# Attention's values, queries and keys as seven products of quarters in place of eight

## The chip, the cores and the metric

The kernel runs on one core of one Trainium2 chip. A core has five engines that run side by side and wait for each other on semaphores: TensorE for matrix products (PE in the profile, its weight loads PEld), VectorE (DVE), ScalarE (ACT), GpSimd (POOL) and SyncE (SP), which here only issues transfers. The metric is the device time of one execution in microseconds (us), less being better.

## The reference, cut to what matters

Two parts follow each other: a graph layer (two rounds of attention over edges) and a transformer block (dense attention, then a mixture of experts). The change touches the dense attention and its border to the graph layer.

```python
def _attention(x, Wqkv, Wproj):          # x: 1 x 1250 x 768, 12 heads of 64
    qkv = (x @ Wqkv).reshape(B, T, 3, H, HD)
    q, k, v = (qkv[:, :, 0], qkv[:, :, 1], qkv[:, :, 2])
    scores = jnp.einsum('bqhd,bkhd->bhqk', q, k) * jnp.float32(HD) ** (-0.5)
    attn = jax.nn.softmax(scores, axis=-1)
    out = jnp.einsum('bhqk,bkhd->bqhd', attn, v).reshape(B, T, D)
    return out @ Wproj
...
x = x + L0_gnn_ref(layernorm(x), ...)          # graph layer
x = x + L0_ffn_ref(layernorm(x)[None], ...)[0]  # x = x + attention(ln1(x)); x = x + moe(ln2(x))
```

All data are float32.

## The kernel before

The 1250 rows are `NT = 10` tiles of `T = 125`, the 768 features `DC = 6` chunks of `P = 128`. A float32 matmul is recorded as two passes of PE.

**End of the graph layer.** `gat_layer(2, ...)` yields row tile after row tile. For each, DVE adds the residual (`xres`), takes two layer norms and leaves `y`; PE turns `y` into six chunks of columns (`ptr`, line 146), and ACT writes them with the norm's scale and offset into `yT` (6 chunks x 1250 columns, in the slot "A" of the pool `big`; slot "B" holds the graph layer's `h`, later the values `v`). With tile 0 the values' weight `wv` (768 x 768) is loaded into the pool `wpool`, which has one buffer. The edge counts `cnt` are read by DVE when it makes the weights `wt` (line 522); PE reads `wt` and `h` in the aggregation (line 529).

**Before the first unit.** POOL fills `zero` and issues nine transfers that clear the table `xd`, which the experts need much later (lines 621 to 627). `value_rows(t)` makes the values of one row tile: two halves of 384 columns, six matmuls each, in a two-bank PSUM tile, copied by ACT (line 663). `queries_keys(p)` makes queries and keys of a pair of heads: it loads the two weight slices `wqk` on SP's queue, and for each of three column chunks of 417 or 416 makes six matmuls for keys (bank `mb`) and six for queries (bank `pz`); ACT copies them into `qk`, scaling the queries by 1/8. It is a generator with one matmul per step. PE's order is written out here (`manual_schedule`): two value tiles, all of pair 0's queries and keys, then the scores of the first unit in turn with the eight other value tiles.

**The units.** A unit is a pair of heads (6) and a third of the queries (3), 18 in all. `Unit.scores(j)` makes the scores of key tile `j` for both heads in a two-bank tile `st` (two buffers); ACT copies them into one of 15 buffers `sT`, DVE keeps the running maximum `most`. `top` and `row` turn the maxima by PE (`ptop`, DVE's reduction `m`, then `mb`). `weights(j)` subtracts on DVE, takes the exponential on ACT, and POOL adds the weights up in `acc`. `values(j)` multiplies with `v` into `pav`. One unit later `divide` sums `acc` over partitions into `pz`, copies `pav` into `aT`, and sends the sums by SP's queue through memory (`zd`, `z`); `invert` takes the reciprocals on DVE and fetches them as `rz` (line 765), and yet a unit later `scale` multiplies on POOL. Only the last unit divides directly. PE's order inside a unit is written out: two steps of the next pair's queries and keys, `top`, `divide`, four steps, the next unit's scores 0, `row`, and then for every two key tiles two scores, two steps (the first three times), and two values. So each of the first fifteen units carries twelve matmuls of the next pair. DVE, ACT, POOL and the transfers are ordered by a planner, apart from instructions pinned with `keep_in_program_order`.

**After the units.** `wp`, the output projection's weight, is loaded into `wpool` once `wv` is done with. `xs`, the rows saved in memory, takes slot "A" after `yT`; its loads alternate between SP's and ACT's queue (line 953). `product(t)` projects row tile `t` (`po`).

Of the kernel before, what the change touches and what calls it, by code (L numbers as in the profile page):

```python
# [10 lines left out]
F32 = mybir.dt.float32  # L11
# [16 lines left out]
def gnn_ffn_kernel(  # L28
# [137 lines left out]
    with tc.tile_pool(name="cnt", bufs=1) as cpool:  # L166
# [277 lines left out]
        with tc.tile_pool(name="gwork", bufs=2) as gp, \  # L444
# [142 lines left out]
            for t, o in gat_layer(2, all_of_second, gb2):  # L587
                if t == 0:
                    yT = big.tile([P, DC, N], F32, tag="A", name="yT")
                    wv = wpool.tile([P, DC, D], F32, tag="w", name="wv")  # L590
                    nc.sync.dma_start(wv, Wqkv[:, 2 * D:3 * D].rearrange("(c p) f -> p c f", p=P))
                xr = gp.tile([T, D], F32, tag="xr", name="xres")
                nc.sync.dma_start(xr, x[t * T:(t + 1) * T, :])
                nc.vector.tensor_add(xr, xr, o)
                nc.scalar.dma_start(xsd[t * T:(t + 1) * T, :], xr)
                mean, rstd = ln_stats(xr)
                nc.vector.tensor_copy(st0[:, 0, t:t + 1], mean)
                nc.vector.tensor_copy(st0[:, 1, t:t + 1], rstd)
                y = gp.tile([T, D], F32, tag="row", name="y")
                ln_apply(y, xr, mean, rstd)  # L600
                mean, rstd = ln_stats(y)
                ln_apply(y, y, mean, rstd)
                transpose_rows(gpt, y, affine(yT, t, 0))


    attn = late.enter_context(tc.tile_pool(name="attn", bufs=1))
    aT = attn.tile([P, DC, N], F32, name="aT")
    with tc.tile_pool(name="att", bufs=2) as ap, \
            tc.tile_pool(name="aps", bufs=2, space=PSUM) as aps, \
            tc.tile_pool(name="apm", bufs=1, space=PSUM) as apm, \  # L610
            tc.tile_pool(name="apa", bufs=1, space=PSUM) as apa:
        heads = [slice(i * HD, (i + 1) * HD) for i in range(2)]
# [4 lines left out]
        def pair_psum(name):  # L617
            return aps.tile([P, 2, 512], F32, tag="s", name=name)


        zero = ap.tile([P, RW], F32, name="zero", bufs=1)
        nc.gpsimd.memset(zero, 0.0)  # L622
        nc.gpsimd.memset(zero[:, D:D + 1], float(NOWHERE))
        for e in range(NE):
            nc.gpsimd.dma_start(xd[e * REG:(e + 1) * REG, :].rearrange("(p r) d -> p r d", p=P),
                                zero[:, None, :].to_broadcast([P, REG // P, RW]))
        nc.gpsimd.dma_start(xd[NOWHERE:NOWHERE + P, :], zero)

        def queries_keys(p):

            wqk = ap.tile([P, DC, 2, P], F32, tag="wqk", name="wqk", bufs=1)
            for i in (1, 0):
                nc.sync.dma_start(wqk[:, :, i, :], Wqkv[:, i * D + p * P:i * D + (p + 1) * P].rearrange(
                    "(c p) f -> p c f", p=P))
            qk = ap.tile([P, 2, N], F32, tag="qk", name="qk")
            yield qk
            for c0, w in CHUNKS:
                for i in (1, 0):
                    if i == 1:
                        pq = apm.tile([P, 2, 512], F32, tag="mb", name="pk")[:, 0, :]  # L640
                    else:
                        pq = apa.tile([P, 512], F32, tag="pz", name="pq")
                    for c in range(DC):
                        nc.tensor.matmul(pq[:, :w], wqk[:, c, i, :], yT[:, c, c0:c0 + w],  # L644
                                         start=(c == 0), stop=(c == DC - 1))
                        if c == DC - 1:
                            nc.scalar.mul(qk[:, i, c0:c0 + w], pq[:, :w], 1.0 if i == 1 else HD ** -0.5)
                        yield None

# [3 lines left out]

        v = big.tile([T, NT, D], F32, tag="B", name="v")

        def value_rows(t):
            pv = pair_psum("pv")
            for s in range(2):
                for c in range(DC):
                    nc.tensor.matmul(pv[:T, s, :DH], yT[:, c, t * T:(t + 1) * T],  # L660
                                     wv[:, c, s * DH:(s + 1) * DH],
                                     start=(c == 0), stop=(c == DC - 1))
            nc.scalar.copy(v[:, t, :].rearrange("p (s d) -> p s d", s=2), pv[:T, :, :DH])

# [8 lines left out]
        def inverses(n):  # L673
            return ap.tile([P, ZW], F32, tag="rz", name="rz")

        class Unit:


            def __init__(self, p, k, qk):
                self.p, self.qk = p, qk  # L680
                self.c0, self.w = CHUNKS[k]
                self.starts = [min(b * BW, self.w - BW) for b in range(NB)]
                self.s = []

            def scores(self, j):
                w = self.w
                st = pair_psum("st")
                for i, r in enumerate(heads):
                    nc.tensor.matmul(st[:T, i, :w], self.qk[r, 1, j * T:(j + 1) * T],  # L689
                                     self.qk[r, 0, self.c0:self.c0 + w], start=True, stop=True)  # L690
                s = ap.tile([T, 2, CW], F32, tag="sT", name="sT", bufs=15)
                nc.scalar.copy(s[:, :, :w], st[:T, :, :w])  # L692
                self.s.append(s)
                if j == 1:
                    self.most = ap.tile([T, 2, CW], F32, tag="most", name="most")
                if j > 0:
# [20 lines left out]
            def weights(self, j):  # L717
                w, s = self.w, self.s[j]
                nc.vector.tensor_tensor(s[:, :, :w], s[:, :, :w], self.mb[:T, :, :w], ALU.subtract)  # L719
                nc.scalar.activation(s[:, :, :w], s[:, :, :w], AF.Exp)  # L720
                if j == 1:
# [47 lines left out]

        steps = queries_keys(0)  # L770
        qks = [next(steps)]
        wp = load_big_weight(Wproj, "wp")
        BEFORE = 2
        with tc.manual_schedule(engines={mybir.EngineType.PE}):
            for t in range(BEFORE):
                value_rows(t)
            for _ in steps:
                pass
            u = Unit(0, 0, qks[0])
            for j in range(NT):  # L780
                u.scores(j)
                if j + BEFORE < NT:
                    value_rows(j + BEFORE)
        units = [(p, k) for p in range(DC) for k in range(NCK)]
        steps = last = None
        waiting = []
        for n, (p, k) in enumerate(units):
            if k == 0:
                steps = None
                if p + 1 < DC:  # L790
                    steps = queries_keys(p + 1)
                    qks.append(next(steps))
            nxt = Unit(*units[n + 1], qks[units[n + 1][0]]) if n + 1 < len(units) else None
            u.ns = NT if nxt is not None else NS
            with tc.manual_schedule(engines={mybir.EngineType.PE}):

                go(steps, 2)
                u.top()
                if last is not None:
                    last.divide(n - 1)  # L800
                for old in waiting:
                    old.scale()
                go(steps, DC - 2)
                if nxt is not None:
# [4 lines left out]
                for j in range(0, NT, 2):  # L809
# [3 lines left out]
                    if j < 6:  # L813
                        go(steps, 2)
                    for i in range(2):
# [388 lines left out]
```

## Time and profile before

| | us |
|---|---|
| median of three runs | 1516.32 (1513.6 to 1520.47) |
| profiled execution | 1515.23 |
| its span, first to last instruction | 1513.5 |
| end of the aggregation to the first unit | 555.5 to 671.7 |
| first fifteen units | 671.7 to 1106 |
| last three units | 1106 to 1177 |

The mean granted clock of TensorE was 0.967 over the span and 1.00 from 560 to 1200 us. Lines of the page that show the sizes of the work concerned (line, engine, operation, output and inputs, shapes, count, then busy us and mean ns of one, then the engine's idle time before them):

```profile
L725 POOL TENSOR_TENSOR acc<-acc,sT 125x834 f32<-125x834 f32 (+1 forms) x139 | 272.9, 1963 | 10.9
...
L644 PE MATMUL pq<-yT,wqk 128*128 128x417 f32 (+1 forms) x216 | 88.1, 534 | 0.0
...
L644 PE MATMUL pk<-yT,wqk 128*128 128x417 f32 (+1 forms) x216 | 84.0, 526 | 0.0
...
L660 PE MATMUL pv<-wv,yT 128*125 128x384 f32 x240 | 79.9, 490 | 1.4 <-issue 1.4
```

The counts are passes, two for a matmul. The three products take 252 us of PE. A mean of one pass includes its drain, which overlaps the next pass; the pace is read from start to start.

### The profile page before, as it was taken

The page shows a single profiled execution, that of the slowest core. Times are in us where ns is not written, and L with a number is a line of the kernel's source. Part 1 is how long each engine was busy: PE and PEld are TensorE (multiplying, and loading weights), DVE is VectorE, ACT ScalarE, POOL GpSimd, SP SyncE. Part 2 cuts the span into 40 slices and gives each one's busy share as a digit, 9 for nine tenths or more (in the row PEclk, how much of TensorE's full clock was granted, in tenths as well). Part 3 has the DMA queues.
Part 4 walks back from the last instruction along what each step waited for, and adds up shares of the span by engine and source line. Part 5 has one row for each costly group of instructions (what it writes and reads, how often), then busy time and mean ns, then how long its engine had stood idle before and what let it go on. Part 6 is the DMA issues. An engine that isn't in the chain of part 4 may idle for free. (4 is left out here: it accounts for less than half of the span.)

```text
span 1513.5 us, 16154 instructions
## 1 busy us (share of the span) xinstructions
PE 1431.7 (95%) x5990; PEld 782.7 (52%) x5990; DVE 756.8 (50%) x1271; ACT 590.3 (39%) x949; POOL 435.2 (29%) x295
## 2 busy tenths in 40 slices
PE   6787999999999999999999999999988999899997
PEld 4584655556555555553344344434333666665654
DVE  6598455435036650117766766766777654111111
ACT  4220613205026521126656656665667123221211
POOL 5000000000000001005765765775676212222222
PEclk9758999999999999999999999999999999899999
DMA  7000020000021119940100101010040323665653
GB/s 208 21 2 11 11 73 0 0 23 10 0 99 45 62 58 382 379 172 1 34 7 6 33 7 28 7 33 7 6 114 10 137 102 137 230 228 172 225 190 122
DMA packets 55578, 128.43 MB, mean 85 GB/s; under 512 B 10797, under 2 KB 29585, under 8 KB 55498
## 3 DMA queue, kind: packets, MB, share of 16 engines
q1 hardware_dynamic: 38846, 61.18, 12.6%
q0 software_dynamic: 11968, 56.21, 10.2%
q10 hardware_dynamic: 4684, 9.99, 2.2%
q8 instruction: 48, 0.79, 0.2%
q14 instruction: 32, 0.26, 0.1%
HBM read 74.17 MB, written 57.66 MB: 87 GB/s over the span
## 5 line engine op out<-in xcount | busy, mean ns | idle before, releaser
L725 POOL TENSOR_TENSOR acc<-acc,sT 125x834 f32<-125x834 f32 (+1 forms) x139 | 272.9, 1963 | 10.9
L529 PE MATMUL pagg<-h,wt 125*125 125x385 f32 (+1 forms) x800 | 263.5, 486 | 0.4 <-DVE wt L522 0.4
L719 DVE TENSOR_TENSOR sT<-sT,mb 125x834 f32<-125x834 f32 (+1 forms) x180 | 174.5, 1013 | 73.9 <-PE mb L714 73.9
L529 PEld LDWEIGHTS pagg<-h,wt 125*125 125x125 f32 x800 | 147.0, 187 | 104.7 <-DVE wt L522 3.5
L698 DVE TENSOR_TENSOR most<-most,st 125x834 f32<-125x834 f32 (+1 forms) x144 | 147.0, 1021 | 105.5 <-ACT sT L692 102.2
L720 ACT ACTIVATE sT<-sT 125x834 f32<-125x834 f32 (+1 forms) x180 | 158.1, 900 | 43.5 <-DVE sT L719 43.0
L692 ACT COPY sT<-st 125x834 f32<-125x834 f32 (+1 forms) x180 | 151.3, 848 | 42.3 <-PE st L689 38.0
L689 PE MATMUL st<-qk 64*125 64x417 f32 (+1 forms) x720 | 162.5, 551 | 5.3 <-DVE most L698 5.2
L733 PE MATMUL pav<-sT,v 125*64 125x417 f32 (+1 forms) x720 | 149.5, 527 | 8.0 <-ACT sT L720 8.0
L622 POOL MEMSET zero<- 128x771 f32 x1 | 0.7, 741 | 530.7 <-PE ptr L146 530.7
L725 POOL TENSOR_TENSOR acc<-sT 125x834 f32<-125x834 f32 (+1 forms) x18 | 35.3, 1963 | 256.5 <-ACT sT L720 256.5
L689 PEld LDWEIGHTS st<-qk 64*125 64x125 f32 x720 | 55.9, 182 | 98.8 <-DVE most L698 52.5
L733 PEld LDWEIGHTS pav<-sT,v 125*64 125x64 f32 x720 | 42.4, 135 | 103.7 <-issue 42.8
L938 PE MATMUL poe<-we,hT 128*128 128x384 f32 x264 | 89.8, 486 | 0.0
L644 PE MATMUL pq<-yT,wqk 128*128 128x417 f32 (+1 forms) x216 | 88.1, 534 | 0.0
L967 PE MATMUL po<-wp,aT 128*125 128x384 f32 x240 | 87.0, 497 | 0.0
L905 PE MATMUL phe<-xT,we 128*128 128x384 f32 (+1 forms) x288 | 86.6, 460 | 0.0
L644 PE MATMUL pk<-yT,wqk 128*128 128x417 f32 (+1 forms) x216 | 84.0, 526 | 0.0
L209 PE MATMUL ph<-gw,xnT 128*125 128x384 f32 x240 | 81.7, 500 | 1.1 <-DMA gw<-in_L_gnn_W_dram 1.1
L660 PE MATMUL pv<-wv,yT 128*125 128x384 f32 x240 | 79.9, 490 | 1.4 <-issue 1.4
L209 PE MATMUL ph<-gw,x1T 128*125 128x384 f32 x240 | 78.6, 488 | 0.0
L533 DVE RECIPROCAL rz<-pagg 125x1 f32<-125x1 f32 x20 | 3.3, 166 | 141.4 <-PE pagg L529 141.4
(230 smaller groups left out, 1699.9 us busy)
## 6 DMA issues: line engine op xcount, KB each, us to landing
xd<-zero POOLq DMA_DIRECT2D x8, 3855.0 KB, 50.2
we<-in_L_ffn_W_dram SPq DMA_DIRECT2D x16, 1152.0 KB
xr<-xd SPq DMA_DIRECT2D x25, 385.5 KB
gw<-in_L_gnn_W_dram SPq DMA_DIRECT2D x2, 2304.0 KB
wqk<-in_L_ffn_Wqkv_dram SPq DMA_DIRECT2D x12, 384.0 KB
xres<-in_x_dram SPq DMA_DIRECT2D x10, 375.0 KB
xsd<-xres ACTq DMA_DIRECT2D x10, 375.0 KB
rz<-zr SPq DMA_DIRECT2D x34, 105.0 KB
```

The lines of the kernel that those rows point to most:

```text
L209: nc.tensor.matmul(po[:, s, :DH], xT[:, c, t * T:(t + 1) * T], w[:, c, s * DH:(s + 1) * DH], start=(c == 0), stop=(c == DC - 1))
L529: nc.tensor.matmul(po[:, s, :DH + s], ws[j][:, (d - d0) * T:(d - d0 + 1) * T], h[:, j, s * DH:(s + 1) * DH + s], start=(j == 0), stop=(j = ...
L644: nc.tensor.matmul(pq[:, :w], wqk[:, c, i, :], yT[:, c, c0:c0 + w], start=(c == 0), stop=(c == DC - 1))
L689: nc.tensor.matmul(st[:T, i, :w], self.qk[r, 1, j * T:(j + 1) * T], self.qk[r, 0, self.c0:self.c0 + w], start=True, stop=True)
L692: nc.scalar.copy(s[:, :, :w], st[:T, :, :w])
L698: nc.vector.tensor_tensor(self.most[:, :, :w], prev[:, :, :w], st[:T, :, :w], ALU.max)
L719: nc.vector.tensor_tensor(s[:, :, :w], s[:, :, :w], self.mb[:T, :, :w], ALU.subtract)
L720: nc.scalar.activation(s[:, :, :w], s[:, :, :w], AF.Exp)
L725: nc.gpsimd.tensor_tensor(self.acc[:, :, :w], prev[:, :, :w], s[:, :, :w], ALU.add)
L733: nc.tensor.matmul(self.pav[r, :w], v[:, j, hd0:hd0 + HD], s[:, i, :w], start=(j == 0), stop=(j == NT - 1))
L938: nc.tensor.matmul(po[:, d, :DH], hT[:, f, s * P:(s + 1) * P], w2[:, f, d * DH:(d + 1) * DH], start=(f == 0), stop=(f == FC - 1))
L967: nc.tensor.matmul(po[:T, s, :DH], aT[:, c, t * T:(t + 1) * T], wp[:, c, s * DH:(s + 1) * DH], start=(c == 0), stop=(c == DC - 1))
```

## The change

A product of two matrices cut in quarters takes eight products of quarters; it can be made with seven (Strassen's scheme in Winograd's form) at the price of sums of quarters before and after. Here the weight's quarters are its upper and lower three chunks by its two halves of output columns (for `wqk`: keys and queries), and the quarters of `yT` its upper and lower three chunks by its first and last five row tiles. Four sums are made of each side's quarters, on POOL: `left_sums` of a weight (pinned, for `wqk`), `right_sums` of two row tiles `t` and `t + 5`. They lie in `t4`, `t2`, `t3`, in place in `yT` and in the weights, and in `aT`, which is not yet in use (`spare`). `seven` makes the products, three matmuls each, and combines them: ACT copies the first product, DVE makes seven additions, the last of which write `v` or `qk`.

What else moves:

- The scale 1/8 goes from the queries into the exponential.
- The last row tile's `y` is written into its place in `v` and is turned by PE between the first two groups of value products, in a bank of the new ring.
- Up to the first unit the products take four PSUM banks in turn (`apq`). In the units they use both banks of `mb` (letters m and n in `BOUND`) and `pz` (z), one product per step.
- POOL's clearing of `xd` comes after the sums of pair 0's weight. Once the values are done, POOL copies `t2` and `t3` into `kept`, which takes `wv`'s buffer; their old place goes to five of the fifteen score buffers. The inverses `rz` lie in `kept`, and for the last units in `yT`.
- `wp` is loaded when the last pair begins.
- Several pools get `reuse_waits="tile"`: memory that a pool takes over is waited for tile by tile.

```diff
-                y = gp.tile([T, D], F32, tag="row", name="y")
+                if t == NT - 1:
+                    v = big.tile([T, NT, D], F32, tag="B", name="v")
+                y = gp.tile([T, D], F32, tag="row", name="y") if t < NT - 1 else v[:, t, :]
...
-    attn = late.enter_context(tc.tile_pool(name="attn", bufs=1))
+    attn = late.enter_context(tc.tile_pool(name="attn", bufs=1, reuse_waits="tile"))
...
+        def left_sums(a, w, flat, pin=False):
+            place = tc.keep_in_program_order if pin else lambda ins: ins
+            s1, s2, s4 = parts(flat, w, 3)
+            a11, a12, a21, a22 = (a[:, c:c + KH, f:f + w] for f in (0, w) for c in (0, KH))
+            place(nc.gpsimd.tensor_tensor(s1, a21, a22, ALU.add))
+            place(nc.gpsimd.tensor_tensor(s2, s1, a11, ALU.subtract))
+            place(nc.gpsimd.tensor_tensor(s4, a12, s2, ALU.subtract))
+            place(nc.gpsimd.tensor_tensor(a21, a11, a21, ALU.subtract))
+            return [a11, a12, s4, a22, s1, s2, a21]
...
+        def right(t2, t3):
+            return [y11, y21, y22, t4, y12, t2, t3]
+        def right_sums(t, t2, t3):
+            q = slice(t * T, (t + 1) * T)
+            nc.gpsimd.tensor_tensor(t3[:, :, q], y22[:, :, q], y12[:, :, q], ALU.subtract)
+            nc.gpsimd.tensor_tensor(y12[:, :, q], y12[:, :, q], y11[:, :, q], ALU.subtract)
+            nc.gpsimd.tensor_tensor(t2[:, :, q], y22[:, :, q], y12[:, :, q], ALU.subtract)
+            nc.gpsimd.tensor_tensor(t4[:, :, q], y21[:, :, q], t2[:, :, q], ALU.subtract)
+        FREE = ["1q", "6q", "2q", "7q", "5q", "4q", "3q"]
+        BOUND = ["1m", "2n", "6z", "7z", "4z", "5m", "3n", "1z", "2z", "6z", "7m", "4n", "5z", "3z"]
...
+        def seven(order, operands, np_, w, o11, o12, o21, o22):
...
+                for c in range(KH):
+                    lhs, rhs = operands(int(i) - 1, c)
+                    nc.tensor.matmul(b, lhs, rhs, start=(c == 0), stop=(c == KH - 1))
...
+                if i == "1":
+                    nc.scalar.copy(p1, b)
+                for o, u in {"2": [(o11, p1)], "6": [(u2, p1)], "7": [(u3, u2)], "4": [(o21, u3)],
+                             "5": [(u4, u2), (o22, u3)], "3": [(o12, u4)]}.get(i, []):
+                    nc.vector.tensor_tensor(o, b, u, ALU.add)
+                yield None
+        QW = -(-NH // 2)
+        PIECES = [(0, QW), (QW, NH - QW)]
...
-                nc.scalar.activation(s[:, :, :w], s[:, :, :w], AF.Exp)
+                nc.scalar.activation(s[:, :, :w], s[:, :, :w], AF.Exp, scale=HD ** -0.5)
...
+            ws = left_sums(wv, DH, spare)
+            for t in range(NU - 1):
+                right_sums(t, t2, t3)
...
+            turns = [iter(value_rows(t, ws, ys)) for t in range(NU)]
+            with tc.manual_schedule(engines={mybir.EngineType.PE}):
+                for _ in turns[0]:
+                    pass
+                for c0 in (0, KH):
+                    pt = free_bank()
+                    for c in range(KH):
+                        nc.tensor.transpose(pt[:, c * P:c * P + T], v[:, NT - 1, (c0 + c) * P:(c0 + c + 1) * P],
+                                            ident[:T, :T])
+                    affine(yT, NT - 1, 0)(c0, KH, pt.rearrange("p (a b) -> p a b", b=P))
+                for _ in turns[1]:
+                    pass
+            right_sums(NU - 1, t2, t3)
...
+            steps = queries_keys(0, ys, True)
...
+                rest = [r for r in turns[2:] for _ in FREE]
+                u = Unit(0, 0, qks[0])
+                for j in range(NT):
+                    u.scores(j)
+                    for r in rest[len(rest) * j // NT:len(rest) * (j + 1) // NT]:
+                        next(r)
+            kept = wpool.tile([P, DC, D], F32, tag="w", name="kept").rearrange("p c d -> p (c d)")
+            ys = right(*parts(kept, NH, 2))
+            nc.gpsimd.tensor_copy(ys[5], t2)
+            nc.gpsimd.tensor_copy(ys[6], t3)
...
-                go(steps, 2)
+                go(steps, 1)
                 u.top()
...
-                go(steps, DC - 2)
+                go(steps, 1)
...
                     if j < 6:
-                        go(steps, 2)
+                        go(steps, 1)
```

## The prediction

> **What bounds the kernel now.** The table of stretches first: it tells which engine is full in the two stages that the change touches. Columns: stretch, its length, busy PE, PEld, DVE, ACT, POOL with instruction counts, granted clock, DMA share, GB/s.
>
> ```profile
> 600.00:640.00 40.00, 40.00 (x127) 21.44 (x126) 4.10 (x4) 7.27 (x9) 0.00 (x0) 1.00 1.02 378
> ...
> 846.39:875.32 28.93, 28.62 (x126) 11.73 (x124) 19.54 (x22) 18.14 (x24) 18.53 (x11) 1.00 0.04 9
> ...
> 1108.28:1133.11 24.83, 19.84 (x101) 7.50 (x101) 19.45 (x21) 17.13 (x23) 17.36 (x10) 1.00 0.33 82
> ```
>
> Up to the first attention unit (600 to 640) PE never stops and the rest idle. A unit that also makes the next pair's queries and keys (846 to 875) takes 28.93 us with PE busy 28.62. A unit without them (1108 on) takes 24.8 (the next 24.2) with PE busy 19.8: there the loop scores, copy, maximum, subtraction, exponential sets the time. So PE bounds fifteen units, and some 4.4 us per unit can be won before the loop takes over.
>
> Next the timeline, for the length of one pass (a float32 matmul is two passes; "x12" is twelve) and for the waits in a unit.
>
> ```profile
> 573.50 4.36 PE L644 MATMUL pk<-yT,wqk 128*128 128x417 f32 x12
> ...
> 599.68 8.01 PE L660 MATMUL pv<-wv,yT 128*125 128x384 f32 x24
> ...
> 1289.61 2.84 PE L905 MATMUL phe<-xT,first_w 128*128 128x256 f32 x12
> ...
> 852.69 0.97 PE L689 MATMUL st<-qk 64*125 64x417 f32 x4
> ...
> 853.59 1.12 PE L714 MATMUL mb<-ident,m 105*125 105x105 f32 x8
> ...
> 855.53 1.67 PE L644 MATMUL pq<-yT,wqk 128*128 128x417 f32 x4
> ...
> 857.13 0.92 PE L733 MATMUL pav<-sT,v 125*64 125x417 f32 x4
> ...
> 860.49 16.27 POOL L725 TENSOR_TENSOR acc<-acc,sT 125x834 f32<-125x834 f32 x8
> ...
> 868.42 1.02 DVE L698 TENSOR_TENSOR most<-most,st 125x834 f32<-125x834 f32 x1 [0.39 <-ACT sT L692]
> ```
>
> The last pass of a run is shown with its drain, so I count start to start: 417 columns (4.36 - 0.51)/11 = 0.350 us, 384 columns (8.01 - 0.49)/23 = 0.327, 256 columns (2.84 - 0.375)/11 = 0.225. Last, the aggregation's end:
>
> ```profile
> 522.30 0.55 DVE L522 SCALAR_TENSOR_TENSOR wt<-e,cnt 125x375 f32<-125x375 f32 x1
> ...
> 549.52 5.99 PE L529 MATMUL pagg<-h,wt 125*125 125x385 f32 x18
> ...
> 555.75 1.02 DVE L535 SCALAR_TENSOR_TENSOR o<-pagg,rz,bias 125x768 f32<-125x768 f32 x1
> ...
> 556.87 6.04 PE L660 MATMUL pv<-wv,yT 128*125 128x384 f32 x18 [1.36 <-issue]
> ...
> 563.16 0.83 PE L146 MATMUL ptr<-ident,y 125*128 125x125 f32 x6 [0.25 <-DVE y L139]
> ...
> 564.11 0.74 POOL L622 MEMSET zero<- 128x771 f32 x1 [530.73 <-PE ptr L146]
> ```
>
> POOL has been free for 530 us, `cnt` is last read at 522.9, `wt` and `h` at 555.5. The profiled execution took 1515.23 us, of which 1513.5 are the span; the median shown is 1516.32, 1.1 more.
>
> **PE, up to the first unit.** Values: 10 tiles x 2 x 6 = 120 matmuls become 5 x 7 x 3 = 105 of the same 384 columns: 15 x 2 x 0.327 = -9.8 us. Queries and keys of pair 0: 3 x 2 x 6 = 36 matmuls of 417 become 2 x 7 x 3 = 42 of 313 or 312. Between the rows for 256 and 384 columns, 313 give 0.225 + 57/128 x 0.102 = 0.270 us a pass: 84 x 0.270 = 22.7 against 72 x 0.350 = 25.2, -2.5. The first product takes a bank of the new ring; today's first started 0.1 us after `o` had been read out of its bank (556.77), so I take the gap of 1.36 as gone (0 to 1.4): -1.3. Sum -13.6.
>
> **What must be ready for it.** The second product needs sums of POOL. Two POOL rows, 417 elements in 0.93 us and 834 in 1.96, give 2.48 ns an element: four sums of 1152 for the values' weight 11.0 us, four of 375 for one pair of row tiles 3.3. The weight was asked for at 416 and `aT`, where the sums lie, takes over the memory of the counts' pool, whose large tile is free at 522.9; rows 5 to 8 are turned by 552. Started at 523, the sums for the first pair are ready long before 557.6, when product two wants them: cost 0. Started only at 555.5 they are ready at 569.8: +12.2. I take 0, since the pools now wait by tile; both ends stay for the range. The last row is turned after the first seven products (21 x 0.65 = 13.7 us, so at 569.4), its `y` being done at 563.0: no wait. Its sums, the memset and the sums of pair 0's weight (3.3 + 0.8 + 4 x 0.85 = 7.5) lie behind the next 13.7 us of products. The nine zero-fill DMAs that held POOL from 565 to 582 now start behind these; only the two copies of `t2` and `t3` stand after them, 75 us later. `wqk` loads on SP from 555.5 on, 20 us ahead of need.
>
> DVE's row chain now has POOL sums beside it, which no row shows. In units, DVE's operations on PSUM keep their 1.0 us with POOL busy or idle, which says 0; but these read SBUF alone, and two sums of 2.7 us on a row that PE awaits say 5.4: I take +1.5.
>
> The Trainium skill speaks against this overlap ("SBUF — State Buffer", section "Who interferes with whom"): a VectorE instruction in a two-port mode and a GpSimd one shut each other out for whole instructions. Our `y` operations (768 elements in 0.68 us, against 0.96 for a two-input add of that size) may well be in such a mode. By the rule, one of the four 2.7 us sums could hold up each of the three rows turned meanwhile, an estimated 8 us instead of 1.5, which would make the time 1501 or 1502; whether it does, this trace cannot show.
>
> The evictions go from ACT to DVE: 35 adds of 384 at 0.56 us and 14 of 313 at 0.49 (line through DVE's PSUM rows of 416 in 0.592 and 834 in 1.02), where DVE was busy 4 of 40 us: hidden, with four banks in turn. If the ring ran dry it would be one add, 0.5 us, per product.
>
> The copies of `t2`, `t3` (1875 elements each) begin when the last value product ends. Per element they cost between the memset (0.96 ns) and the add (2.48): 3.6 to 9.3 us for both. The new score buffers lie where `t2`, `t3` were and are first written some 5.3 us into unit 0; ACT's copy waits there, with the exponentials behind it: 0 to 4, I take +1.5.
>
> **PE, in the fifteen units.** Before: 12 matmuls, 8.4 us, in five runs that measured 1.51 + 3.00 + 3 x 1.60 = 9.31. After: 14 products per three units, each 6 x 0.270 = 1.62. Per pair 36 x 0.70 = 25.2 becomes 22.7, and one run less saves its change of 0.2: -2.7, five pairs -13.6. The second run, halved, covered the maximum (1.20 us on DVE after `ptop`): `pz` 0.85, the product 1.62 and `st` 0.9 still do. `mb` shares its bank with the products before it and now waits for a DVE add (0.5) rather than an ACT copy (0.52); `st` covers either.
>
> DVE gains 14 adds per pair, 6.9 us, 2.3 a unit beside 19.5. Where it is packed (854.8 to 868.0, 13.2 us of work while PE takes 14.1) three adds come in, 1.47; PE's three products there are 0.22 longer each, so the room is 0.9 + 0.66 = 1.53. It fits barely: 0 to 1.47 a unit, I take 0.2, +3.0. ACT is relieved of two copies of 0.52 a unit and given two of 0.42 per pair. POOL gets 4 x 0.85 = 3.4 every third unit, in the 9.8 us that it idles before the first `acc`; `wqk` is free one step earlier than today, so SP has brought it by then. `acc` ends 1.1 us ahead of `pz` today; both shift alike.
>
> **Tail.** `wp` loads some 50 us before its use: 0. `xs` takes the slot of `yT`, which now holds the last inverses: its loads move from 1099 behind the last `scale` (1175.5 in today's time). The ACT stalls on these loads (2.4 + 1.0 + 2.5 us) cost units 14 and 15 about 0.8: won. Row 0 is wanted at 1180.7; at 382 GB/s, this trace's best slice, a row of 375 KB takes 1 us and landing some 2 more: in time. If the two loads of `first_w` (2.3 MB, 6 us) go first, or ACT waits on its triggers, 0 to +8. I take +1.0.
>
> **Sum.** -13.6 + 1.5 + 1.5 - 13.6 + 3.0 - 0.8 + 1.0 = -21.0: 1494.2 for the profiled execution, and with the median's 1.1 about **1495**. With every term at its good end 1484.
>
> **Rivals.**
> 1. Late sums (wait for `wt`, not for `cnt`): 1495 + 12.2 = 1507. For it: the zero memset waited for the last turn although `zero` needed only space. Against: the pools' new rule.
> 2. Late `xs`: +8, 1503. For: ACT already stalled on these triggers. Against: PE has two rows of `po` ahead, about 16 us.
> 3. The adds move the bound: each of 14 sits on PE's path, because banks `mb` and `pz` are single and DVE is in order: 14 x 0.49 = 6.9 per pair in place of 0.6, +31, **1526, slower**. It decides from 1.6 us of stall per unit on. For: DVE full from 854.8 to 868, and `st` waits for `most` there (41.7 us in all, mostly hidden). Against: 3.7 us lie between two products of one bank.
> 4. The shorter passes do not come shorter (0.350): six pairs +4.2 in place of -2.5, +40, 1535. Against: 256 columns did take 0.225.
>
> **Chances.** Forecast 0.62 (its own range 1484 to 1505), late sums 0.14, late `xs` 0.09, adds on the path 0.12, passes 0.03. A measurement of this kernel tells some 0.5%, 7.6 us, from no change: faster means below 1508.7, slower above 1523.9. Faster: 0.62 + two thirds of the first rival + most of the second = 0.79; same 0.09; slower 0.12. The range 1483 to 1512 leaves out the third and fourth rival and a little of the first.
>
> **What would show it.** Passes of 0.27 us; first unit starting near 658, not 671.7; unit period 28.0 to 28.3, not 28.93, and 24.2 to 24.8 unchanged without products; the second product without a wait at about 557.6; first `y` of the projection on `xs` some 20 us earlier. A wait of PE for POOL at 558 is rival 1; PE waiting for DVE adds at `mb` or `pz` over 1.6 us a unit is rival 3. I'm wrong if the period does not fall.

## The result, and the profile after

The changed kernel takes 1501.18 us (median of four runs, 1500.91 to 1505.32) against 1518.39 (1513.6 to 1522.37) for the kernel before beside it: the ratio is 0.9896, 95% interval [0.9865, 0.9926], 17 us less. The forecast was 1495.

The whole span is a poor measure of a single part here. The graph layer ahead of the attention is the same code in all kernels of this study, yet the moment at which it has read its edge counts for the last time (end of the last `wt`, line 522) lies anywhere between 519.6 and 528.3 us in fourteen profiles. So everything below is measured from that moment on, between marks that every timeline shows: the end of the aggregation (last `pagg`), the first maximum of unit 0 (DVE's reduction `m`), the maximum of each next unit, the last maximum, the end of the span. Profiled executions, us:

| stretch | before | before, again | after | after, again | forecast of the difference |
|---|---|---|---|---|---|
| last read to end of aggregation | 32.7 | 32.7 | 34.8 | 34.8 | +1.5 |
| to first maximum | 119.6 | 119.6 | 103.9 | 103.9 | -13.6 |
| unit 0 | 29.3 | 29.3 | 33.5 | 34.1 | +0.8 |
| units 1 to 14 | 405.0 | 404.8 | 398.0 | 396.3 | -10.7 |
| units 15 and 16 | 49.0 | 50.2 | 50.0 | 49.2 | 0 |
| last maximum to the end | 355.1 | 355.2 | 353.7 | 357.6 | +1.0 |
| sum | 990.6 | 991.7 | 973.9 | 975.9 | -21.0 |

The forecasts of the fifteen units (-13.6 + 3.0) are spread evenly here; the copies' +1.5 stand with unit 0 and the -0.8 of the loads with units 1 to 14. Two profiles of one kernel agree within 0.6 us up to unit 0; after it they differ by up to 4, so that a tail's gain of 1 or 2 us cannot be read from the end of the span. Part of that scatter is TensorE's granted clock. Of the tail, the table of stretches shows for the change, for the change again and for the kernel before (length, then busy time and count of PE, PEld, DVE, ACT, POOL, granted clock, DMA share, GB/s):

```profile
1255.00:1300.00 45.00, 35.58 (x172) 27.48 (x171) 12.54 (x62) 13.25 (x32) 15.24 (x17) 0.89 0.43 146
1255.00:1300.00 45.00, 35.55 (x157) 27.61 (x155) 11.77 (x57) 13.25 (x32) 14.06 (x16) 0.81 0.42 140
1270.00:1315.00 45.00, 36.01 (x170) 28.61 (x169) 12.54 (x61) 13.97 (x35) 14.66 (x17) 0.81 0.45 157
```

The clock stood at half for 10 us of these 45 in the first profile of the change and for 17 us in the other two (twice 0.11 and twice 0.19 of 45). So of the two tails 357.6 is the one to compare with 355.1, and the change costs the tail some 2.5 us, which the 353.7 hides.

The timeline of PE in the changed kernel (start, us, engine, line, operation, count of passes), from the end of the aggregation:

```profile
556.65 3.72 PE L529 MATMUL pagg<-h,wt 125*125 125x385 f32 x11
560.20 2.10 PE L684 MATMUL q<-wv,yT 128*125 128x384 f32 x6
562.14 2.10 PE L684 MATMUL q<-aT,t 128*125 128x384 f32 x6
...
573.75 0.81 PE L849 MATMUL q<-ident,v 125*128 125x125 f32 x6
...
589.52 1.75 PE L684 MATMUL q<-t,aT 128*128 128x313 f32 x6
591.10 1.74 PE L684 MATMUL q<-yT,wqk 128*128 128x313 f32 x6
```

The first product starts where the aggregation ends, the second follows without a wait, the last row tile is turned without one either. Six passes of 384 columns follow each other in 1.94 us, 0.323 each; six of 313 in 1.58, 0.263 each. So 35 products for the values take 67.9 us, where 240 passes of 0.327 had taken 78.5 (-10.6); 14 products for queries and keys take 22.1, where 72 of 0.350 had taken 25.2 (-3.1); and the gap of 1.4 is gone. That is 15.1 of the 15.7 us that this stretch became shorter.

One pair of heads later, units 3 to 5 in the table of stretches (columns as above), each from PE's first product in it to PE's first in the next:

```profile
752.21:779.93 27.72, 27.58 (x130) 12.46 (x128) 21.39 (x26) 17.71 (x23) 22.41 (x15) 1.00 0.03 9
779.93:808.16 28.23, 28.09 (x132) 12.86 (x130) 21.56 (x27) 17.55 (x23) 18.65 (x11) 1.00 0.04 9
808.16:837.13 28.97, 27.16 (x128) 12.19 (x126) 21.36 (x27) 17.04 (x22) 18.83 (x11) 1.00 0.13 36
```

PE is full in the first two. The third carries four products in place of five, but PE idles for 1.8 us of it. Its two largest waits, from PE's timeline:

```profile
814.06 0.97 PE L752 MATMUL st<-qk 64*125 64x417 f32 x4 [0.58 <-DVE qk L691]
829.68 0.97 PE L752 MATMUL st<-qk 64*125 64x417 f32 x4 [0.96 <-DVE most L762]
```

Product 4 gives the queries that the next unit's first scores read; PE makes the two one after the other, and DVE's addition lies between. The periods from maximum to maximum show it throughout: 28.2, 28.2, 28.5 where they were 28.9.

Unit 0, in contrast, became longer. The timeline of all engines (only the lines spoken of):

```profile
661.59 1.74 POOL L878 COPY kept<-t 128x1875 f32<-128x1875 f32 x1
...
663.30 0.99 POOL L639 TENSOR_TENSOR aT<-wqk 128x384 f32<-128x384 f32 x1
...
668.82 5.57 ACT L784 ACTIVATE sT<-sT 125x834 f32<-125x834 f32 x6 [3.68 <-DVE sT L783]
670.73 1.96 POOL L789 TENSOR_TENSOR acc<-sT 125x834 f32<-125x834 f32 x1 [6.44 <-ACT sT L784]
672.64 0.86 POOL L640 TENSOR_TENSOR aT<-aT,wqk 128x384 f32<-128x384 f32 x1
...
673.56 1.93 PE L684 MATMUL pq<-kept,aT 128*128 128x313 f32 x3 [4.94 <-POOL aT L640]
...
674.30 0.84 ACT L756 COPY sT<-st 125x834 f32<-125x834 f32 x1
```

The second of the next pair's four left sums (line 640) stands on POOL behind the first `acc`, which waits 6.4 us for an exponential. PE needs that sum at 668.6 and gets it at 673.5. ACT, too, copies no scores of unit 1 between 663.3, when the copy of `t3` has freed their memory, and 674.3: six exponentials stand first.

PE's wait was not the whole loss. Unit 0 from maximum to maximum, before and after the change, and 6.8 us of it after the change:

```profile
675.12:704.44 29.32, 27.85 (x122) 11.35 (x122) 19.48 (x20) 19.15 (x24) 17.68 (x9) 1.00 0.09 34
...
664.23:697.75 33.52, 28.54 (x128) 13.45 (x128) 22.27 (x26) 18.03 (x22) 20.24 (x13) 0.90 0.26 96
670.17:676.99 6.82, 3.43 (x6) 1.84 (x7) 6.82 (x8) 6.68 (x9) 6.26 (x5) 0.50 0.37 137
```

From 670.2 to 677.0 the granted clock was 0.50, and the three passes in the PE line above took 1.93 us; at full clock six take 1.85 (the next experiment shows the line). All eight profiles of this study in which PE waits over 4 us in unit 0 show 6.8 us at half clock there, beginning 1.5 to 3.4 us after PE stopped; the six others show none. No run has the wait without the slow clock, so the two are not priced apart.

### The profile page after: what moved, and what is told of

Read it like the earlier page. It is cut to its first block, busy times and chain, and to the rows that moved or that the text cites. A ratio compares the mean times of both kernels' runs of the same rounds, so it can differ in the third digit from the quotient of the medians.

```text
span 1499.4 us, 16427 instructions
## 1 busy us (share of the span) xinstructions
PE 1407.0 (94%) x6032; PEld 791.8 (53%) x6032; DVE 813.4 (54%) x1390; ACT 572.1 (38%) x920; POOL 490.1 (33%) x345
## 5 line engine op out<-in xcount | busy, mean ns | idle before, releaser
L789 POOL TENSOR_TENSOR acc<-acc,sT 125x834 f32<-125x834 f32 (+1 forms) x139 | 273.0, 1964 | 10.7
L1008 ACT ACTIVATE hT<-phe 128x384 f32<-128x384 f32 (+2 forms) x30 | 13.1, 437 | 155.5 <-PE phe L1006 155.5
L1006 PEld LDWEIGHTS phe<-xT,we 128*128 128x128 f32 x288 | 52.1, 190 | 33.6
L1043 DVE SCALAR_TENSOR_TENSOR sofar<-poe,weight,sofar 128x768 f32<-128x768 f32 x23 | 23.4, 1018 | 82.5 <-PE poe L1039 82.5
```

The lines of the kernel that those rows point to most:

```text
L789: nc.gpsimd.tensor_tensor(self.acc[:, :, :w], prev[:, :, :w], s[:, :, :w], ALU.add)
L1006: nc.tensor.matmul(ph[:, :n * P], w1[:, c, f * P:(f + 1) * P], xT[:, c, :], start=(c == 0), stop=(c == DC - 1))
```

## The experiments

### The change and the kernel before, once more

> The changed kernel once more, unedited. Its profiled execution had three losses besides the change's own arithmetic: everything stood 2.7 us later already at the last read of the edge counts (525.5 against 522.9), and PE lost some 1.8 us each in unit 14 and unit 16 with no wait that the trace names. If these are accidents of one execution, this profile has the counts' last read within 1 us of 522.9 and units 14 and 16 at about 28.5 and 24.5 us, and the time is 1497 to 1500. If they belong to the changed program, they stand at the same places and the time is about 1501.

> The kernel before, once more, for its marks. If they lie within 1 us of the profile before, the marks of single profiles can be compared: last read of the edge counts 522.8, from there to the end of the aggregation 32.7, first maximum at 675.1, units of 28.9, last maximum to the end 355.1. If the last read lies near 525 instead, the 2.7 us by which it was later in the changed kernel were no part of the change.

The change took 1501.86 us (1500.1 to 1505.88), ratio 0.9905 [0.9884, 0.9926]; the kernel before, in its one run, 1517.98. The marks are in the table above. The last read of the counts came at 524.1 and 524.5 us, where the first two profiles had 525.5 and 522.8: the 2.7 us by which it was later after the change were scatter. Unit 14 of the first profile, 30.0 us, took 28.4 in the second, unit 16 24.0 rather than 26.0. Unit 14 in the first and the second profile:

```profile
1065.68:1095.71 30.03, 26.52 (x120) 11.03 (x122) 21.07 (x26) 17.04 (x22) 18.50 (x10) 0.94 0.03 8
1064.88:1093.27 28.39, 24.88 (x120) 10.75 (x122) 21.08 (x26) 17.04 (x22) 18.54 (x10) 1.00 0.05 9
```

The clock was at half for 3.4 us of the longer one, and again in unit 16; in the second profile such a stretch falls in unit 15. In all fourteen profiles, a unit 14 of over 29.3 us and a unit 16 of over 25.5 are those that hold one. So the long units were accidents, as the first branch of the expectation had it, and yet the time stayed at 1501.9, its second branch. Unit 0 took 34.1: that was no accident.

### The left sums of pair 1 ahead of unit 0

```diff
+            later = right(None, None)
+            ahead = queries_keys(1, later, False)
+            qks.append(next(ahead))
...
-                if p + 1 < DC:
+                if p == 0:
+                    steps = ahead
+                elif p + 1 < DC:
```

> The loading and the four POOL sums of pair 1's weight are put ahead of the last value products, so that they lie before unit 0's additions of weights on POOL. Theory (PE's 4.9 us wait in unit 0 comes from POOL taking the first addition of weights, which waits for an exponential, ahead of the second sum, which the waiting product needs): the wait goes, unit 0 takes 28.5 to 29.5 us from maximum to maximum in place of 33.6, and the time falls by 4 to 5 us against the changed kernel. Rival (unit 0 is slow because of the two copies of 1.74 us each, whatever the order): it stays above 31.5 us.

1500.35 us (1499.45 to 1504.71), ratio 0.9891 [0.9871, 0.9911], unit 0 34.2: the gain did not come, though POOL now had its sums ready. Timeline:

```profile
665.80 0.85 POOL L641 TENSOR_TENSOR aT<-wqk,aT 128x384 f32<-128x384 f32 x1
...
670.23 1.85 PE L684 MATMUL pq<-kept,aT 128*128 128x313 f32 x6
670.50 6.50 ACT L784 ACTIVATE sT<-sT 125x834 f32<-125x834 f32 x7 [3.68 <-DVE sT L783]
...
676.90 1.59 ACT L756 COPY sT<-st 125x834 f32<-125x834 f32 x2
...
677.79 1.76 PE L752 MATMUL st<-qk 64*125 64x417 f32 x4 [4.16 <-ACT sT L756]
```

The product runs without a wait, and PE then stops for 4.2 us at the scores, and again its clock is at half for 6.8 us, from 676.7 on (the four passes of `st` take 1.76 us in place of 0.97): both buffers `st` are full, and ACT empties them only after seven exponentials, although `t3` had been copied away at 665.8. There were two waits behind one another; by these lines both come from the order in which POOL's and ACT's work around the memory of `t2` and `t3` was planned, and taking one away uncovered the other.

### The copies of t2 and t3 on VectorE

```diff
-            nc.gpsimd.tensor_copy(ys[5], t2)
-            nc.gpsimd.tensor_copy(ys[6], t3)
+            nc.vector.tensor_copy(ys[5], t2)
+            nc.vector.tensor_copy(ys[6], t3)
```

> The change as it is, with the two copies of t2 and t3 into kept on VectorE in place of GpSimd (order of the engines: the copies now stand just ahead of the first maximum reduction, the left sums of the next pair are the first thing on GpSimd, and ScalarE's score copies of unit 1 are mixed with its exponentials from the second one on). Theory (unit 0 loses 4 to 6 us only through the order in which GpSimd and ScalarE were given the work around the memory of t2 and t3): unit 0, maximum to maximum, falls from 33.5-34.1 to 28.2-30; the first maximum comes up to 3.3 us later (two copies of 1875 columns, 1.66 us each at the rate of the 125x768 VectorE rows of 0.68 us), so unit 0 and the offset together win 2 to 5.5 us: 1496 to 1499.5. Rival (the loss of unit 0 is the first exponentials' own, whatever the order): unit 0 stays over 33 and the time is 1501 or more.

1493.69 us (1489.3 to 1499.08), ratio 0.9836 [0.9807, 0.9865]. Unit 0 took 28.8, the first maximum was not later (103.9 as before the edit), all other units stayed. Unit 0 in the table of stretches, and the timeline:

```profile
664.82:693.67 28.85, 27.40 (x128) 12.41 (x128) 22.08 (x27) 17.97 (x22) 17.66 (x9) 1.00 0.52 186
...
660.92 1.13 DVE L877 COPY kept<-t 128x1875 f32<-128x1875 f32 x1
...
661.97 1.13 DVE L878 COPY kept<-t 128x1875 f32<-128x1875 f32 x1
...
667.37 0.85 ACT L756 COPY sT<-st 125x834 f32<-125x834 f32 x1 [2.94 <-PE st L752]
...
669.14 1.58 PE L684 MATMUL pq<-kept,aT 128*128 128x313 f32 x5
```

The clock stayed at 1.00. ACT now copies the first scores of unit 1 as soon as they are there, ahead of any exponential; the left sums of the next pair were done on POOL before the copies. The copies themselves cost nothing seen: they fill DVE's time while PE makes the last products. This edit changes who copies and, through the planner, the order on three engines; what it shows is that unit 0's loss belongs to this place. That the order, not the length of a POOL copy, was the cause rests on the timelines: with the copies on POOL their memory was free 11 us before ACT wrote it. No run keeps the copies on POOL and changes ACT's order alone.

### Three of seven additions left out in the units

```diff
+                if few:
+                    adds = {"2": [(o11, p1)], "4": [(o21, p1)], "5": [(o22, p1)], "3": [(o12, p1)]}
```

> In the units, three of each seven additions on DVE are left out (the ones that only make running sums), and the other four add the first product in place of the running sum: queries and keys from pair 1 on are not the reference's, and the experts' work behind may change, so only the units are read. DVE loses 2 x 0.48 us a unit. If DVE sets the pace where the adds fall (theory: in every third unit, which has no product in the last slot, and not in the others), the third unit gets 0.5 to 1 us shorter and the other two stay within 0.2 us; three units take 84.0 to 84.4 us in place of 84.9. If PE alone bounds, all stay: 84.9. If adds are on PE's path everywhere, three units take 82 us or less.

1500.6 us in one run. Units 1 to 14 took 394.7, against 396.3 in the comparable profile: three additions fewer in each half, 30 in all for ten halves of five pairs, are worth 1.6 us. They came from where the theory looked, in a smaller size: the third unit of a pair took 28.1 rather than 28.5 in four pairs of five, the other two units stayed, and three units took 84.5. PE's wait for `qk` (2.9 us in five pairs) stayed, since product 4's own addition stayed.

### Values alone as seven products

```diff
-            ws = left_sums(wqk, P, spare[:, (4 + p % 2) * N:], pin=True)
...
+            for c0, w in CHUNKS:
+                for i in (0, 1):
...
+                    for c in range(DC):
```

> Values by seven products as in the changed kernel, queries and keys by eight as before (pair 0 in the ring of four banks, the rest two, four and three times two matmuls a unit). By the terms of the sum: the stretch from the end of the aggregation to the first unit takes 116.2 - 9.8 - 1.4 = 105 us in place of 101.3; unit 0 has no wait for POOL; the units are back at 28.9 us. Time against the changed kernel: +2.5 (pair 0) + 15 x 0.6 - 4.5 (unit 0) = about +7 us, 1505 to 1508. If instead most of the gain came from the queries and keys, the stretch would be near 111 us or more.

1505.72 us (1504.12 to 1509.65), ratio 0.992 [0.9895, 0.9945]. To the first maximum 106.8 in place of 103.9: the seven products of pair 0 are worth 2.9 us there and those of the values, with the gap, 12.8. Unit 0 took 29.3 and the next ones 28.9, as before the change. So queries and keys as seven products won 8 us in units 1 to 14 (404.2 to 396.3), and with them came the loss of 4 to 5 in unit 0.

### Product 4 one slot earlier, twice

```diff
-        BOUND = ["1m", "2n", "6z", "7z", "4z", "5m", "3n", "1z", "2z", "6z", "7m", "4n", "5z", "3z"]
+        BOUND = ["1m", "2n", "6z", "7z", "4z", "5m", "3n", "1z", "6z", "7m", "4n", "2z", "5z", "3z"]
```

and, in the second kernel,

```diff
+        BOUND = ["1m", "2n", "6z", "7z", "4z", "5m", "3n", "1z", "6z", "7z", "4m", "2n", "5z", "3z"]
```

> The change with the second half's products in the order 1 6 7 4 2 5 3 rather than 1 6 7... 2 first (1 2 6 7 4 5 3), so that product 4, which gives the queries that the next unit's first scores read, ends one slot earlier, and product 2 takes its slot. Theory (in the third unit of a pair PE waits for the VectorE add behind product 4): the waits of st for qk fall from 2.9 us in all to under 0.5, three units from 84.9 to about 84.3, five pairs -2.9 us: 1498 to 1499. Rival (the same idle time passes to the maximum chain, st for most): three units stay at 84.9 and the time at 1501-1502.

> The change with the second half's products in the order 1 6 7 4 2 5 3, as in the run before, but with banks so that no product asks for the pair of banks that still holds the broadcast maxima: 1, 6 and 7 in the single bank, 4 and 2 in the pair, which is free where 4 starts. Theory (the loss of the other order was the bank, and the wait of the scores for product 4's VectorE add can be had for nothing): waits of st for qk under 0.5 us in all, no wait of a product for VectorE's subtraction, three units 84.3 rather than 84.9, five pairs -2.9 us: 1498 to 1499.5. Rival (the idle time of the third unit passes to the maximum chain, or products in the single bank wait for the copy of the denominators): three units 84.9 or more, 1501 or more.

The first order took 1509.74 us (1504.54 to 1511.48), ratio 0.994 [0.9918, 0.9963]: 8 us worse than the change. The view of waits of PE, units 1 to 16 (total us, times, longest), has in the change

```profile
PE st L752 <- DVE qk L691: 2.9, 5, 0.6
...
```

and no wait of a product for a bank, and in this kernel:

```profile
PE mq L684 <- DVE sT L783: 8.7, 5, 1.7
PE st L752 <- DVE most L762: 7.3, 9, 1.0
PE pq L684 <- ACT zs L817: 3.0, 5, 0.6
...
```

The wait for `qk` is gone, but product 7 now asks for the pair of banks `mb` one slot sooner, while DVE still subtracts the maxima that lie there; and product 2 asks for `pz` before ACT has copied the denominators out. Neither theory had this. The second order gives both products other banks. It took 1497.19 us (1490.71 to 1506.02), ratio 0.9856 [0.9824, 0.9888]. Its four times spread over 15 us, so the view of waits over the same stretch, and the periods, decide:

```profile
PE st L752 <- DVE most L762: 7.3, 9, 1.0
PE pav L797 <- ACT sT L784: 4.2, 5, 1.2
...
```

No wait for `qk` and none for a bank; the third unit takes 27.8 rather than 28.5 in four pairs of five, while the wait for `most` stays as it was. In the fifth pair it takes 29.4, with 3.4 us at half clock in it; units 1 to 14 together took 395.1, and from the last read to the end 976.0, no less than the change. So in this profile the gain stands in the units and not yet in the whole.

### The sums of the values' weight in short pieces

```diff
-            place(nc.gpsimd.tensor_tensor(s1, a21, a22, ALU.add))
+            for c in [slice(None)] if pin else [slice(c, c + 1) for c in range(KH)]:
+                place(nc.gpsimd.tensor_tensor(s1[:, c], a21[:, c], a22[:, c], ALU.add))
```

> The change with the four left sums of the value weights in three pieces of 384 columns each, twelve GpSimd operations for four. Theory (a VectorE row operation that starts beside a GpSimd sum ends only when that sum ends, so that the row chain waits up to 2.6 us for one): no 125x768 row operation on VectorE above 1.6 us, and the stretch from the last read of the edge counts to the end of the aggregation falls from 34.8 to 33-33.8 us (before: 32.7). Rival (GpSimd's share slows VectorE by the same sum, however cut): the longest falls, but more operations are slowed and the stretch stays at 34.5 or more.

1502.19 us in one run. The stretch from the last read to the end of the aggregation took 33.8, at the edge of what the theory expected: 1.0 of the 2.2 us came back. What held a row operation up is plain in the change's own timeline:

```profile
525.76 2.62 POOL L639 TENSOR_TENSOR aT<-wv 128x1152 f32<-128x1152 f32 x1 [489.97 <-DVE wt L522]
...
526.19 2.60 DVE L139 TENSOR_SCALAR y<-y,mv,rstd 125x768 f32<-125x768 f32 x1
...
528.94 0.30 PE L146 MATMUL ptr<-ident,y 125*128 125x125 f32 x1 [1.25 <-DVE y L139]
```

The operation `y`, 0.68 us long elsewhere, starts 0.43 us after POOL's sum and ends 0.4 us after that sum has ended. In pieces of 384 the same operation took 0.98. One prediction of the theory failed: `xres` beside the last tile's right sums still took 1.71 us. Those sums are of 375 columns, no longer than the pieces, so short sums do not free an addition with both inputs in SBUF. And one later `y` rose from 0.68 to 1.09 us: POOL's right sums, which had ended before it in the change, now ran beside it.

### The last inverses elsewhere, so that xs can load early

```diff
-            return yT.rearrange("p c n -> p (c n)")[:, at:at + ZW]
+            if n == len(units) - NCK:
+                self_rz.append(ap.tile([P, DC, 2 * P], F32, tag="wqk", name="rz", bufs=1))
+            return self_rz[0].rearrange("p c n -> p (c n)")[:, at:at + ZW]
```

> The change with the last three units' inverses in the buffer of the weights wqk, dead by then, rather than in that of the sums' rows yT, so that the loads of xs need not wait for the last scale. Theory (the term of the late xs, +1.0 us): the wait of about 14 us on xs at ScalarE goes, the first norm's square root comes some 2 us earlier after the last maximum, and the stretch from the last maximum to the first transpose of the projection falls from 32.5 to 30.3-31.5 us. Rival (hidden): the loads come earlier, that stretch stays at 32 or more, and the tail at 354 to 358.

1497.94 us in one run. From the last maximum to the first transpose of the projection: 30.3 before the change, 32.5 and 32.9 after it, 30.35 here. ACT's timeline of the change,

```profile
1172.80 1.28 ACT L129 ACT_TABLE_LOAD   x1 [14.19 <-DMA xs<-xsd]
1174.10 0.30 ACT L129 ACTIVATE sd<-mv,eps 125x1 f32<-125x1 f32 x1
```

and of this kernel:

```profile
1092.17 0.51 ACT L821 COPY zs<-pz 128x416 f32<-128x416 f32 x1 [2.40 <-DMA xs<-xsd]
...
1153.53 1.28 ACT L129 ACT_TABLE_LOAD   x1
1167.74 0.29 ACT L129 ACTIVATE sd<-mv,eps 125x1 f32<-125x1 f32 x1 [12.93 <-DVE yn L1085]
```

After the change ACT waits in the queue's triggers until 1172.8, and only then loads the table and takes the first root. With early loads the table is loaded in the shadow of PE's last work. The stretch is 2.2 to 2.5 us shorter, as the theory had it, but the tail took 356.0, within the rival's range, and from the last read to the end 975.4, like the change (973.9 and 975.9): the low time goes with an early last read, at 520.8. ACT now waits 2.4 us for triggers at 1090, in unit 14, which took 30.0 us here. That is no price of the edit as far as is shown: 3.4 us of this unit, from 1082.5 on, were at half clock, and the last kernel below has the same edit and a unit 14 of 27.8.

### Together

> The change with the copies of t2 and t3 on VectorE and the second half's products in the order 1 6 7 4 2 5 3 with 1, 6, 7 in the single bank and 4, 2 in the pair. Both won in different units (5 us in unit 0, 0.7 us in the third unit of each of five pairs), so the sum should hold: unit 0 28.8, the third units 27.8, about 1490 us, ratio 0.981 to 0.984. Rival (one cover for both): 1493 or more.

> As the run beside it, and in addition the left sums of the value weights in pieces of 384 columns (-1 us on the row chain) and the last three inverses in the buffer of wqk (first transpose of the projection 2 us earlier after the last maximum, for up to 1.6 us of stall at ScalarE in the last pair). Theory (these are terms of their own): 1.3 us below the run beside it, 1488.5. Rival (the pieces' gain is lost again before the end): the same time as the run beside it within 1 us.

With VectorE's copies and the second order of products: 1493.55 us (1489.26 to 1495.69), ratio 0.9842 [0.9818, 0.9866]; unit 0 28.9, third units 27.8, units 1 to 14 393.1, and 967.9 us from the last read of the counts to the end, 6 to 8 less than the change. With short sums and early `xs` in addition: 1489.42 us (1485.73 to 1493.8), ratio 0.9817 [0.9791, 0.9843]; 33.8 to the end of the aggregation in place of 34.8, the first transpose 30.35 after the last maximum in place of 32.5, units 1 to 14 393.1, 964.5 from the last read to the end. In the marks the terms add up; the medians of the two kernels are 4 us apart with intervals that overlap, so that the last two parts are shown by marks and not by the time. The last kernel is the best of the study, with an interval of its ratio that lies below that of the change. The medians hide part of it: the first kernel of this pair did not beat VectorE's copies alone (1493.69), though its units were 3.3 us shorter, so by its time the rival (1493 or more) came true and by its units the theory.

## Why the prediction was right, and where it was wrong

The direction and the mechanism were right and the time was inside the range, 6 us above the forecast. Point by point:

- **PE up to the first unit**, -13.6: -15.7 measured. The pass of 313 columns, put between two rows at 0.270, took 0.263, that of 384 0.323, and the gap went. The first unit nevertheless started at 661.6, not 658, since the stretch began 4.9 us later: 2.7 of scatter ahead of it, 2.2 of the row chain.
- **Readiness of the sums**: the second product had no wait, POOL's first sum was released by the last `wt`. Rival 1 fell on the first profile.
- **Row chain beside POOL**, +1.5 of 0 to 5.4: +2.2. The Trainium skill ("SBUF — State Buffer", section "Who interferes with whom") had the mechanism, a lock for whole instructions; the row that I weighed against it, DVE's operations on PSUM beside POOL, did not bear on operations that read and write SBUF alone. The estimate of 8 us made from the rule was too high, since one and not three of these operations fell under a long sum: 2.60 us in place of 0.68. The same section has an instruction with two inputs in SBUF contend with GpSimd's reads, which `xres` shows with 1.71 us for 0.96.
- **Copies of t2 and t3**, +1.5 of 0 to 4: this step failed. It priced the copies' length and the wait for their memory; the copies took 3.5 us and nobody waited long for them. What cost 4 to 5 us was, by the timelines, the order in which sums, `acc`, exponentials and score copies stood on POOL and ACT: PE waited 4.9 us, and 6.8 us of the unit ran at half clock, for which the sum had no term. I had read the order of PE, which is written out, and taken the planned order of the others as given by readiness.
- **Fifteen units**, -13.6 + 3.0: in the first two units of each pair -0.7, as forecast; in the third only -0.5, because of the bare addition between product 4 and the scores (0.6 us). I had looked for adds in the packed part of DVE's unit and not for an eviction whose reader stands next on PE. Of the other additions, leaving out 30 won 1.6 us, where the sum had 3.0 for all of them together.
- **Stalls of ACT on the loads of xs**, -0.8: before the change unit 14 is 0.1 to 0.2 us above its neighbours, so there was no more to win there; units 15 and 16 together show nothing beyond their scatter.
- **Late xs**, +1.0: 2.2 to 2.5 us to the first transpose, through the table load and the root behind the triggers, a smaller form of rival 2. The first `y` of the projection came 13 and 16 us earlier in the two profiles, not 20. The tail itself took 2.5 us more at a like clock; that the table's mean shows +0.5 is luck, as one of its tails had 7 us less at half clock.
- **Rival 3**, adds on PE's path at 1.6 us a unit: PE waited for additions 0.6 us per pair. **Rival 4**: the passes did come shorter.
- **The good end, 1484**, does not come out of the terms as given: the gap at its full 1.4 and the row chain, the copies, the additions and the late `xs` all at nothing give 1488.

The sum of the table is -16.3 us against -21.0 forecast: unit 0 is 3.7 of the difference, units 1 to 14 are 2.9 (0.8 of it the half clock in one unit 14), the row chain 0.7; the stretch up to the first maximum gives 2.1 back and the tail 0.5. So errors of both signs met in a time that lay inside the range.

## What to carry to other kernels

Price a product by its columns, start to start, and the length of its passes comes out within a few per cent (0.270 us forecast, 0.263 measured); the gain of the engine is less sure, so look for what stands directly behind each evicted result in that engine's order, because there an addition of half a microsecond is paid in full. Where memory changes hands, read the planned order of the engines beside it: work that is ready in time may still stand behind something that is not, and moving the hand-over to another engine can be worth more than making it earlier. An earlier slot for one product is only free if its bank is. Read the granted clock beside every stretch that is longer than it should be.

## What was not expected of the hardware

- A VectorE operation of 0.68 us that starts beside a GpSimd sum lasts 2.60 us, to 0.4 us past the sum's end. Two-input additions of rows in SBUF (`xres`) rose from 0.96 to between 1.05 and 1.71 beside GpSimd sums. The groups of DVE from the last read of the counts to the last tile's rows (busy us, mean ns), in the change:

```profile
L139 DVE TENSOR_SCALAR y<-y,mv,rstd 125x768 f32<-125x768 f32 x3 | 4.0, 1317 | 0.1
L594 DVE TENSOR_TENSOR xres<-xres,o 125x768 f32<-125x768 f32 x3 | 3.9, 1312 | 0.1
L535 DVE SCALAR_TENSOR_TENSOR o<-pagg,rz,bias 125x768 f32<-125x768 f32 x3 | 3.1, 1018 | 0.1
```

  and in the kernel before:

```profile
L535 DVE SCALAR_TENSOR_TENSOR o<-pagg,rz,bias 125x768 f32<-125x768 f32 x3 | 3.1, 1018 | 0.1
L594 DVE TENSOR_TENSOR xres<-xres,o 125x768 f32<-125x768 f32 x3 | 2.9, 957 | 0.1
L139 DVE TENSOR_SCALAR y<-y,mv,rstd 125x768 f32<-125x768 f32 x4 | 2.7, 679 | 0.1
```

  The operation that reads PSUM, `o`, keeps its 1018 ns.
- A copy of 1875 columns within SBUF takes 1.74 us on GpSimd and 1.13 on VectorE.
- From 135 us on, TensorE's granted clock drops to half for 3.4 to 10.2 us at a time. In unit 0 it does so in each of the eight profiles in which PE waits over 4 us, and in no other; elsewhere the place changes from one execution to the next, and 3.4 us of it cost unit 14 1.6 us.
- The same code up to the last read of the edge counts ends 8.7 us apart in different executions, while the stretches after it up to the first maximum repeat within 0.1 us.
